# Row LSTM over group-normalised images: held row transfers, unread products tied to statistics, and a last step in two parts

## The chip, the core and the metric

The kernel runs on one core of a Trainium2 chip. A core has TensorE (matrix products, results in PSUM banks), VectorE, ScalarE, GpSimd (all three elementwise, GpSimd without access to PSUM) and SyncE, whose queue here issues every DMA. The metric is the device time of one launch in microseconds (us); lower is better. Six runs of the kernel before gave a median of 2072.43 us, from 2069.31 to 2076.78.

## The reference

`x` has 8 images of 96 channels, 128 rows, 128 columns, in float32. It is group-normalised over whole images (32 groups of 3 channels), and a row LSTM goes down the rows: a masked convolution of the normalised row, plus a convolution of the previous hidden row, gives four gates.

```python
def step(carry, row_in):
    h, c = carry
    ss = lax.conv_general_dilated(h, W_ss, window_strides=(1,), padding=((1, 1),), ...) + b_ss[None, :, None]
    gates = ss + row_in
    g5 = gates.reshape(B, 3, 4, Oc, Wd)
    f = jax.nn.sigmoid(g5[:, :, 0].reshape(B, O, Wd))
    i = jax.nn.sigmoid(g5[:, :, 1].reshape(B, O, Wd))
    o = jax.nn.sigmoid(g5[:, :, 2].reshape(B, O, Wd))
    g = jnp.tanh(g5[:, :, 3].reshape(B, O, Wd))
    c_new = f * c + i * g
    h_new = o * jnp.tanh(c_new)
    return ((h_new, c_new), h_new)
...
x = x + _L0_conv_ref(_gn(x), ...)
```

No hidden row can begin before the statistics of its image are complete, and the rows of one image follow each other.

## The kernel before

**Two halves.** The 8 images are two sets of four (`s` = 0 and 1). A half-step is one row of one set, so there are 256 of them, taken in turn: half-step `n` is row `n // 2` of set `n % 2`. One set's elementwise work runs while TensorE multiplies for the other. Each row is split into even and odd columns and the convolution is done with sums and differences: `vs` (total), `vf` (difference), `vd` (shifted differences) come from the hidden row with the last 32 normalised channels below it (`hx`); `xs` holds the same three for the first 64 channels.

**First stage: the statistics.** The loop at L700 to L728 reads each image as six chunks of 128 partitions x 2048 (1 MB; the last chunk in two halves) into a ring of six buffers, and VectorE runs `bn_stats` on 512 columns at a time (L724). Chunks 2 and 4 of an image are summed by ScalarE instead (`sums_of`, L209). The counter `m` counts pieces of 512, and `events` holds what is issued after piece `at(image, n)`: the whole preparation of half-steps 0 and 1 is written between the statistics of images 3 to 7. All engines but SyncE run in the order in which the program is written (`manual_schedule`); SyncE issues DMAs in program order too.

For set 1 the scale of its first three images is made at `at(7, 5)` to `at(7, 8)`; `next_row` (L625) normalises row 0 of these on GpSimd, `next_operands` (L631) makes their `vs`, `vf`, `vd` on GpSimd, and `own_row` at `at(7, 20)` their `xs`. The last image's scale can only follow the last `bn_stats`: `aggregate(7)`, then L735 to L744 (small matmuls L245 for deviations, variances and means, a Newton iteration for the reciprocal root on VectorE), then L745 to L758 for its row 0.

**Unread products.** `spin(count, rhs)` (L169) issues matmuls of 128 x 256 into a PSUM bank that nothing reads. There are 11 at `at(7, 8)` and 4 at L740, each of two passes on TensorE.

**Row transfers.** After the statistics loop SyncE issues, in this order: rows 1 to 3 of set 1 (`load_rows(1, 0, 1, R)` at L731: two transfers of 384 KB into the first and the last 64 partitions of `xr[1]`; `load(1, 0, 1, R)`: 192 KB and 576 KB into `x`), and then rows of the next block of four: `load_rows(0, 1)`, `load` of both sets, `load_rows(1, 1)` (L765 to L768). None of the first four waits for compute. ScalarE widens rows 1 to 3 of `xr[1]` (L761), GpSimd normalises their shared channels (L762) and combines them (L764); half-step 3 is the first to use the result.

**Second stage.** `do(1, ...)` at L771 begins the recurrent products, and the loop at L772 issues `PERIOD` for each `n`; a prime marks work of the half-step before. A half-step's last part is `gated` (i*g), `cell` (f*c + i*g), `cell_tanh`, `output`, and `residual` with the store in `finish`.

Of the kernel before, what the change touches and what calls it, by code (L numbers as in the profile page):

```python
# [8 lines left out]
AF = mybir.ActivationFunctionType  # L9
# [6 lines left out]
def strided(ap, offset, dims):  # L16

    return bass.AP(ap.tensor, ap.offset + offset, [ap.ap[0], *[list(d) for d in dims]])
# [3 lines left out]
def kernel(  # L22
# [32 lines left out]
    nc = tc.nc  # L55
    B, C, H, W = x.shape
    P = 128
    NH = 2
    BH = B // NH
# [25 lines left out]
    wt = [tap[1], wm[:, 0, :], wm[:, 1, :], tap[2]]  # L85
# [39 lines left out]
    xr = [const.tile([P, BH, R * W], F32, tag=f"xr{s}", name=f"xr{s}") for s in range(NH)]  # L125
# [3 lines left out]
    xw = [const.tile([P, R, W + 1], F32, tag=f"xw{i}", name=f"xw{i}") for i in range(2)]  # L129
# [21 lines left out]
    def load(s, k, lo=0, hi=R, copy=True):  # L151
        if lo == 0:
            xt[s, k] = x_pool.tile([P, BH, R, W], F32, tag=f"x{s}", name=f"x{s}_{k}")
        flat = xt[s, k].rearrange("c b r w -> c b (r w)")[:, :, lo * W : hi * W]
        if copy:
            nc.sync.dma_start(flat[C:P], rows_of(s, k, C2, C, lo, hi))
        nc.sync.dma_start(flat[0:C], rows_of(s, k, 0, C, lo, hi))
# [7 lines left out]
    def bank(name):  # L165
        return ps_pool.tile([P, 512], F32, tag="ps", name=name)


    def spin(count, rhs):  # L169
        unread = bank("spin")  # L170
        for i in range(count):
            nc.tensor.matmul(  # L172
                unread[:, 0 : rhs.shape[1]],
                wt[0][:, 0:P],
                rhs,
                start=True,
                stop=True,
                skip_group_check=True,
            )
# [113 lines left out]
    def widen(engine, xw, i, n, s, k, j, lo, step=1):  # L293


        norm(
            engine,
            strided(xw[:, i, :], 0, [(step * (W + 1), n), (J + 1, 2), (1, J)]),
            (x0[:, 0, j] if s == 1 and k == lo == 0 else xr[s][:, j, lo * W : (lo + n) * W])
            .rearrange("p (r j t) -> p r t j", r=n, t=2),  # L300
            0,
            1,
            s * BH + j,
        )

    def combine(xw, n, total, differences):

        e, o = xw[:, 0:n, 0:J], xw[:, 0:n, J + 1 :]
        nc.gpsimd.tensor_add(total, e, o)  # L309
        nc.gpsimd.tensor_sub(  # L310
            differences,
            strided(xw[:, 0, :], 0, [(W + 1, n), (J, 2), (1, J)]),
            strided(xw[:, 0, :], J + 1, [(W + 1, n), (0, 2), (1, J)]),
        )
# [7 lines left out]
    def own_row(xw, s, r, lo=0, hi=BH):  # L322

        to = xs[s][0]
        combine(
            xw[:, lo:hi],
            hi - lo,
            to[:, r, 0, lo:hi],
            to[:, r, 1:3, lo:hi].rearrange("p t b j -> p b t j"),
        )  # L330
# [24 lines left out]
    class HalfStep:  # L355
# [89 lines left out]
            to = self.g if self.row > 0 else self.c  # L445
            nc.vector.tensor_mul(to, self.ps[1][0:C], self.g)  # L446

        def cell(self):
            if self.row > 0:
                nc.vector.tensor_add(self.c, self.ps[0][0:C], self.g)  # L450

        def cell_tanh(self):
            self.th = self.tile("th")
            nc.scalar.activation(self.th, self.c, AF.Tanh)  # L454

        def output(self):
            s, row = self.s, self.row
            nxt = hx[s][(row + 1) // R % 2][0:C, (row + 1) % R]
            self.h = strided(nxt[:, 0, 0, :], 0, [(BH * JP + 1, 2), (JP, BH), (1, J)])
            shaped = "p (t b j) -> p t b j"  # L460
            nc.vector.tensor_mul(
                self.h,
                self.ps[2][0:C].rearrange(shaped, t=2, b=BH),
                self.th.rearrange(shaped, t=2, b=BH),
            )


        def operand(self, name, parts=1):
# [37 lines left out]
    def store(s, k, lo, hi):  # L506
        nc.sync.dma_start(
            out[s * BH : (s + 1) * BH, :, k * R + lo : k * R + hi, :].rearrange(
                "b c r w -> c b (r w)"
            ),  # L510
            xt[s, k][0:C, :, lo:hi, :].rearrange("c b r w -> c b (r w)"),
        )
# [21 lines left out]
    def work(n):  # L534
        if n < len(FIRST):
            return FIRST[n]
        row, s = divmod(n, NH)
        k, r = divmod(row, R)
        parts = []
        if r == R - 1 and k + 2 < NB:  # L540
            parts.append((own_image, s, k + 2, 0))
        elif r < R - 1 and k + 1 < NB:
            parts.append((own_image, s, k + 1, r + 1))
        if k + 1 < NB:
            parts += shared(s, k + 1, *SHARED[r])
        if r == R - 2 and k + 2 < NB:
            parts.append((load_rows, s, k + 2))
        return parts

    def finish(n):  # L550
        for part, *args in work(n):
            part(*args)
        row, s = divmod(n, NH)
        k, r = divmod(row, R)
        if r == R - 1:
            store(s, k, R - 1 if k + 1 == NB else 0, R)
            if k + 2 < NB:
                load(s, k + 2)
        elif r == R - 2 and k + 1 == NB:
            store(s, k, 0, R - 1)  # L560
# [19 lines left out]
    last = NT * NH - 1  # L580

    def half_step(n):
        if n not in steps:
            steps[n] = HalfStep(n)
        return steps[n]

    def do(n, names):

        for name in names.split():
            at = n  # L590
            for mark, offset in (("'", -1), ("+", 1), ("*", 2)):
                if mark in name:
                    at, name = n + offset, name.replace(mark, "")
            tile_ = name[-1] if name[-1] in order else ""
            part = name[: len(name) - len(tile_)]

            if part in ("S", "F", "D"):
                at += NH
            if not 0 <= at <= last:
                continue  # L600
            step = half_step(at)
            if name not in step.done:
                step.done.add(name)
                getattr(step, PARTS[part])(*([order[tile_]] if tile_ else []))
# [15 lines left out]
    def shared_rows(engine, s, lo, hi, images=range(BH)):  # L620
        for j in images:
            normalise_shared(engine, s, 0, j, lo, hi)


    def next_row():  # L625
        late[0].scale()
        late[0].shift()
        for j in range(BH - 1):
            widen(nc.gpsimd, xw[1], j, 1, 1, 0, j, 0)

    def next_operands():  # L631
        shared_rows(nc.scalar, 1, 0, 1, range(BH - 1))
        step = half_step(1)
        step.total(nc.gpsimd, 0, BH - 1)
        step.difference(nc.gpsimd, 0, BH - 1)
        step.shifted(0, BH - 1)

# [12 lines left out]
    def at(image, n):  # L650
        return image * NS + n
# [9 lines left out]
    def squares():  # L661
        late[0].squares()
        late[0].variances(late[0].q)
        late[0].means()


    events = {
        at(3, 1): lambda: first_rows(0, (0,)),
# [14 lines left out]
        at(6, 22): lambda: first_rows(1),  # L683
        at(7, 5): lambda: (late.insert(0, Scale(1, BH - 1, BH)), begin_scale(1, 0, BH - 1)),
        at(7, 6): squares,
        at(7, 8): lambda: (next_row(), spin(11, wt[0][:, 0:256])),
        at(7, 12): next_operands,
        at(7, 20): lambda: own_row(xw[1], 1, 0, 0, BH - 1),
    }
    for b in range(B - 1):  # L690
        events[at(b + 1, 7 if b == 4 else 4)] = lambda b=b: aggregate(b)
# [7 lines left out]
    n = m = 0  # L699
    for b in range(B):  # L700
        bst = g_pool.tile([P, NS, 6], F32, tag="bst", name=f"bst{b}")
# [4 lines left out]
        done = 0  # L706
# [30 lines left out]
    final.variance_and_square()  # L737
    final.variances(final.q)
    final.means()
    spin(4, wt[0][:, 0:256])  # L740
    nc.scalar.activation(final.minus, final.pm, AF.Identity, scale=-1.0)
    final.scale()
    nc.gpsimd.tensor_mul(final.nmr, final.minus, final.rstd)
    j = BH - 1  # L744
# [8 lines left out]
    step = half_step(1)  # L753
# [15 lines left out]


    do(1, "1A 2A 1B 2B PA PB QA QB PC P+A QC")  # L771
    for n in range(1, last + 2):  # L772
        for names in PERIOD:
            do(n, PRODUCTS[n % 2] if names == "X" else names)
            if "re'" in names.split():
                finish(n - 1)


# [53 lines left out]
```

## Time and profile before

The profiled execution took 2073.84 us; its span, from the first to the last instruction, is 2071.6 us.

| Quantity | Value |
|---|---|
| Median of 6 runs | 2072.43 us (2069.31 to 2076.78) |
| Profiled execution, time | 2073.84 us |
| Profiled execution, span | 2071.6 us |
| TensorE busy, share of the span | 1953.6 us, 94% |
| VectorE, GpSimd, ScalarE busy | 81%, 70%, 66% |
| Mean granted TensorE clock | 0.993 |
| First statistics to the last `bn_stats` | until 137.1 us |
| Recurrent products on TensorE | about 144 to 2064 us |

The page gives busy times and shares of each engine, the chain of work that ended last, and the costliest groups of instructions. Other views list instructions in order of time with the idle time before them and what ended it (in square brackets), or busy time, granted TensorE clock and DMA rate in stretches of the span. A granted clock of 1.00 is full speed, 0.50 half. In a row such as `L724 DVE ... x4`, L724 is the line of the program, DVE is VectorE, ACT ScalarE, POOL GpSimd, PE TensorE, and SPq SyncE's queue; PEld is TensorE loading weights.

### The profile page before, as it was taken

What the parts mean: (1) busy time and instruction counts of PE and PEld (TensorE: products, weight loads), DVE (VectorE), ACT (ScalarE), POOL (GpSimd) and SP (SyncE); (2) the same over time, 40 slices, a digit from 0 to 9 for tenths busy, and PEclk for the clock granted to TensorE, in tenths of its full rate; (3) what the DMA queues carried; (4) which work ended last, traced back from release to release, by engine and by line L of the source; (5) the groups of instructions that cost most, each with busy time, mean ns of one, the idle gap of its engine ahead of it and who ended that gap; (6) DMA issues with size and microseconds to landing.
All of it is one profiled execution on the core that took longest, in us unless ns stands there. A gap on an engine that the chain in (4) does not pass through costs nothing.

```text
span 2071.6 us, 31323 instructions
## 1 busy us (share of the span) xinstructions
PE 1953.6 (94%) x10832; PEld 1594.9 (77%) x10832; DVE 1678.0 (81%) x3491; ACT 1359.9 (66%) x2397; POOL 1443.7 (70%) x1645
## 2 busy tenths in 40 slices
PE   0259999999999999999999999999999999999998
PEld 0248888888888888888888888888888888888886
DVE  4768888888888888888888888888888888888887
ACT  4756666666666666666666666666666666666666
POOL 2347777777777777777777777777777777777762
PEclk9979999999999999999999999999999999999999
DMA  9993333444333344433334443333444333344411
GB/s 370 421 314 81 88 88 98 112 112 109 76 81 92 92 112 113 112 80 79 88 92 112 112 113 90 76 80 92 112 112 112 92 78 85 87 108 112 112 31 31
DMA packets 103324, 236.24 MB, mean 114 GB/s; under 512 B 5952, under 2 KB 8896, under 8 KB 97280
## 3 DMA queue, kind: packets, MB, share of 16 engines
q1 hardware_dynamic: 103168, 234.25, 41.4%
q8 instruction: 87, 1.43, 0.3%
q14 instruction: 69, 0.57, 0.1%
HBM read 183.90 MB, written 50.33 MB: 113 GB/s over the span
## 4 chain that ended last, share of the span: by engine, by line
PE 93%; DMA 4%; DVE 1%; POOL 0%; ACT 0%; SPq 0%; issue 0%; DVEq 0%; POOLq 0%
PE ps L378 93%; DMA xs<-in_x_dram 4%; DVE bst L724 1%; PE spin L172 0%; POOL xw L291 0%; POOL xs L310 0%; SPq L712 0%; POOL xs L309 0%; ACT xs L216 0%; ACT xs L215 0%; ACT g L430 0%; PE dm L245 0%; DVE g L446 0%; DVE c L450 0%; DVE st L654 0%
## 5 line engine op out<-in xcount | busy, mean ns | idle before, releaser
L378 PE MATMUL ps<-vd,wl 128*128 128x256 f32 x3072 | 815.6, 388 | 0.0
L430 ACT ACTIVATE g<-ps 32x512 f32<-32x512 f32 x768 | 453.7, 591 | 453.0 <-PE ps L378 444.6
L378 PEld LDWEIGHTS ps<-vd,wl 128*128 128x128 f32 x3072 | 563.7, 190 | 150.3 <-issue 85.4
L486 POOL TENSOR_TENSOR vd<-hx 128x512 f32<-128x512 f32 x257 | 266.2, 1036 | 469.2 <-DVE vs L478 466.2
L378 PE MATMUL ps<-xs,wx 64*128 64x256 f32 x3072 | 457.9, 395 | 10.7 <-POOL xs L309 10.7
L378 PE MATMUL ps<-vs,wm 128*128 128x256 f32 x1536 | 458.8, 381 | 0.0
L378 PE MATMUL ps<-vf,wm 128*128 128x256 f32 x1536 | 458.4, 380 | 0.0
L437 ACT ACTIVATE ps<-ps 96x512 f32<-96x512 f32 x766 | 417.5, 572 | 16.4 <-PE ps L378 0.3
L378 PEld LDWEIGHTS ps<-xs,wx 64*128 64x128 f32 x3072 | 323.4, 187 | 118.5 <-issue 84.4
L442 DVE TENSOR_TENSOR ps<-ps,c 96x512 f32<-96x512 f32 x254 | 176.8, 696 | 261.6 <-ACT ps L437 261.6
L427 DVE TENSOR_TENSOR ps<-m,ps 128x256 f32<-128x256 f32 x768 | 329.3, 429 | 26.4
L423 DVE TENSOR_TENSOR ps<-m,ps 128x256 f32<-128x256 f32 x768 | 325.3, 424 | 9.4 <-ACT m L420 0.7
L504 POOL TENSOR_TENSOR x<-x,hx 96x512 f32<-96x512 f32 x254 | 328.7, 1294 | 0.0
L378 PEld LDWEIGHTS ps<-vs,wm 128*128 128x128 f32 x1536 | 293.2, 191 | 40.2 <-POOL vs L478 0.7
L378 PEld LDWEIGHTS ps<-vf,wm 128*128 128x128 f32 x1536 | 293.0, 191 | 39.6 <-DVE vf L482 0.3
L420 ACT ACTIVATE m<-ps,wl 128x256 f32<-128x256 f32 x513 | 243.2, 474 | 77.1 <-PE ps L378 63.6
L310 POOL TENSOR_TENSOR xs<-xw 128x512 f32<-128x512 f32 (+1 forms) x254 | 269.9, 1063 | 0.0
L378 PE MATMUL ps<-xs,wt 64*128 64x256 f32 x1536 | 264.9, 377 | 0.1
L454 ACT ACTIVATE th<-c 96x512 f32<-96x512 f32 x256 | 161.2, 630 | 106.2 <-DVE c L450 105.1
L291 POOL TENSOR_SCALAR hx<-x,rstd,nmr 32x512 f32<-32x512 f32 (+1 forms) x252 | 203.4, 807 | 25.9
L378 PEld LDWEIGHTS ps<-xs,wt 64*128 64x128 f32 x1536 | 195.3, 187 | 18.4 <-issue 1.0
L291 POOL TENSOR_SCALAR xw<-xr,rstd,nmr 128x512 f32<-128x512 f32 x252 | 203.6, 808 | 7.0 <-DVE nmr L283 6.5
(84 smaller groups left out, 1283.0 us busy)
## 6 DMA issues: line engine op xcount, KB each, us to landing
xr<-in_x_dram SPq DMA_DIRECT2D x124, 512.0 KB, 6.4
x<-in_x_dram SPq DMA_DIRECT2D x63, 768.0 KB, 5.8
out_dram<-x SPq DMA_DIRECT2D x62, 768.0 KB, 4.7
xs<-in_x_dram SPq DMA_DIRECT2D x30, 1024.0 KB, 12.4
piece<-in_x_dram SPq DMA_DIRECT2D x16, 1024.0 KB, 12.4
x<-in_x_dram SPq DMA_DIRECT2D x62, 256.0 KB, 3.1
xs<-in_x_dram SPq DMA_DIRECT2D x4, 512.0 KB, 8.5
out_dram<-x SPq DMA_DIRECT2D x2, 576.0 KB, 3.7
```

The lines of the kernel that those rows point to most:

```text
L291: engine.tensor_scalar(dst, src, scale, shift, ALU.mult, ALU.add)
L310: nc.gpsimd.tensor_sub(differences, strided(xw[:, 0, :], 0, [(W + 1, n), (J, 2), (1, J)]), strided(xw[:, 0, :], J + 1, [(W + 1, n), (0, 2) ...
L378: nc.tensor.matmul(self.ps[a][:, bass.ts(half, HB)], weights[rows, bass.ts(a, P)], rhs[rows], start=new, stop=False, skip_group_check=True,)
L420: nc.scalar.activation(self.m1[a], m1, AF.Identity, bias=column)
L423: nc.vector.tensor_add(self.ps[a][:, 0:HB], self.m1[a], self.ps[a][:, HB:])
L427: nc.vector.tensor_sub(hi, self.m1[a], hi)
L430: nc.scalar.activation(self.g[a * 32 : (a + 1) * 32], self.ps[a][C:P], AF.Tanh)
L437: nc.scalar.activation(gate, gate, AF.Sigmoid)
L442: nc.vector.tensor_mul(f, f, self.c)
L454: nc.scalar.activation(self.th, self.c, AF.Tanh)
L486: diff = nc.gpsimd.tensor_sub(self.operand("vd", 2)[:, :, lo:hi], strided(h, 1, [(BH * JP - 1, 2), (JP, hi - lo), (1, J)]), strided(h, 0, ...
L504: (nc.gpsimd if row + 1 < NT else nc.vector).tensor_add(xo, xo, self.h)
```

## The change

Three parts, each at its own place.

- `next_operands` gets a GpSimd write of one column of zeros into `xr[1]`, behind the `total` of that step. The column is the first of row 1, so `load_rows(1, 0, 1, R)`, which writes over it, waits for it; GpSimd's `difference` and `shifted` come after it.
- The unread products at `at(7, 8)` go from 11 to 8. `keep_warm(count)` issues one product that reads the newest record of `bn_stats` (6 columns), in a bank of its own, and `count` products of the old kind in another. It is called with 2 at `at(7, 20)`, 2 at `at(7, 22)` and 1 at `at(7, 24)`: behind the last `bn_stats` of chunk 4, and of each half of chunk 5. The unread products at L740 go from 4 to 2.
- The half-step loop ends one turn earlier. What the last turn did for the last half-step is written out: the same products, sigmoids, tanhs and `gated`, then `cell` and `cell_tanh` for images 0 and 1 and for images 2 and 3, then `output` in the same two parts, `residual` and `finish`.

The built program's order agrees: TensorE has the new products in these places, GpSimd one Memset between `vs` and `vf`, the first row transfer waits for GpSimd, and the last half-step has two instructions each in place of one on VectorE (`c`, `hx`) and ScalarE (`th`). The order of all else is the same.

```diff
+        def part(self, ap, lo, hi):
+            return ap.rearrange("p (t b j) -> p t b j", t=2, b=BH)[:, :, lo:hi]
+
-        def cell(self):
+        def cell(self, lo=0, hi=BH):
             if self.row > 0:
-                nc.vector.tensor_add(self.c, self.ps[0][0:C], self.g)
-
-        def cell_tanh(self):
-            self.th = self.tile("th")
-            nc.scalar.activation(self.th, self.c, AF.Tanh)
-
-        def output(self):
+                c, f, g = (self.part(ap, lo, hi) for ap in (self.c, self.ps[0][0:C], self.g))
+                nc.vector.tensor_add(c, f, g)
+
+        def cell_tanh(self, lo=0, hi=BH):
+            if lo == 0:
+                self.th = self.tile("th")
+            nc.scalar.activation(self.part(self.th, lo, hi), self.part(self.c, lo, hi), AF.Tanh)
+
+        def output(self, lo=0, hi=BH):
...
-            shaped = "p (t b j) -> p t b j"
-            nc.vector.tensor_mul(
-                self.h,
-                self.ps[2][0:C].rearrange(shaped, t=2, b=BH),
-                self.th.rearrange(shaped, t=2, b=BH),
-            )
+            o, th = (self.part(ap, lo, hi) for ap in (self.ps[2][0:C], self.th))
+            nc.vector.tensor_mul(self.h[:, :, lo:hi], o, th)
...
         step.total(nc.gpsimd, 0, BH - 1)
+        nc.gpsimd.memset(xr[1][:, 0, W : W + 1], 0.0)
         step.difference(nc.gpsimd, 0, BH - 1)
...
+    def keep_warm(count):
+        spin(1, bst[:, done - 1, :])
+        spin(count, wt[0][:, 0:256])
...
-        at(7, 8): lambda: (next_row(), spin(11, wt[0][:, 0:256])),
+        at(7, 8): lambda: (next_row(), spin(8, wt[0][:, 0:256])),
         at(7, 12): next_operands,
-        at(7, 20): lambda: own_row(xw[1], 1, 0, 0, BH - 1),
+        at(7, 20): lambda: (own_row(xw[1], 1, 0, 0, BH - 1), keep_warm(2)),
+        at(7, 22): lambda: keep_warm(2),
+        at(7, 24): lambda: keep_warm(1),
...
-    spin(4, wt[0][:, 0:256])
+    spin(2, wt[0][:, 0:256])
...
-    for n in range(1, last + 2):
+    for n in range(1, last + 1):
         for names in PERIOD:
             do(n, PRODUCTS[n % 2] if names == "X" else names)
             if "re'" in names.split():
                 finish(n - 1)
+    do(last, "siB fg taB 3C 0C taC siC gt")
+    step, halves = half_step(last), [(0, BH // 2), (BH // 2, BH)]
+    for at in halves:
+        step.cell(*at)
+        step.cell_tanh(*at)
+    for at in halves:
+        step.output(*at)
+    step.residual()
+    finish(last)
```

## The prediction, made before the changed kernel ran

> **What bounds the kernel now.** I read the engine shares first, then the chain of work that ended last, then the stretches where that chain is not TensorE's steady work. The page's summary of the chain:
>
> ```profile
> PE 93%; DMA 4%; DVE 1%; POOL 0%; ACT 0%; SPq 0%; issue 0%; DVEq 0%; POOLq 0%
> ```
>
> 93% is one unbroken run of matmuls, from about 144 us to 2058 us. The change leaves it alone. What can move is when that run starts and the 13 us behind it. The chain around the start (start, duration, what):
>
> ```profile
> 120.89 14.91 DMA xs<-in_x_dram
> ...
> 135.82 1.30 DVE bst L724 x2
> ...
> 137.21 0.68 DVE st L654
> ...
> 138.03 0.57 PE dm L245 x2
> ...
> 138.62 0.29 DVE q L266
> ...
> 138.96 1.02 PE pv L245 x4
> 139.98 0.85 PE dm L245 x4
> 140.83 3.42 PE spin L172 x8
> 144.25 5.79 PE ps L378 x31
> ```
>
> The start is held in three places: by the last image transfer, by small matmuls for the last image's scale, and by the four unread products (eight passes, 3.42 us). VectorE's timeline shows the first:
>
> ```profile
> 131.16 1.29 DVE L724 BATCH_NORM_STATS2 bst<-xs 128x6 f32<-128x512 f32 x2 [0.41 <-DMA xs<-in_x_dram]
> 132.88 1.29 DVE L724 BATCH_NORM_STATS2 bst<-xs 128x6 f32<-128x512 f32 x2 [0.43 <-DMA xs<-in_x_dram]
> 135.82 1.28 DVE L724 BATCH_NORM_STATS2 bst<-xs 128x6 f32<-128x512 f32 x2 [1.66 <-DMA xs<-in_x_dram]
> ```
>
> These are the last chunks' statistics. The first 512 KB half of the last chunk is there at 132.88, the second only at 135.82. Why, and what TensorE's clock does, stands in the table by stretches (us, busy time of PE, PEld, DVE, ACT, POOL, granted clock, DMA share, GB/s):
>
> ```profile
> 120.00:126.00 6.00, 2.07 (x10) 2.04 (x10) 5.87 (x13) 1.94 (x4) 0.26 (x1) 0.50 1.01 421
> ...
> 131.00:137.00 6.00, 2.63 (x13) 1.97 (x11) 3.75 (x6) 3.09 (x6) 3.93 (x10) 1.00 1.09 208
> ```
>
> ```profile
> 133.67:137.09 3.42, 0.00 (x0) 0.00 (x0) 1.76 (x3) 0.51 (x2) 2.07 (x8) 1.00 1.08 198
> 137.09:140.50 3.41, 2.10 (x10) 2.04 (x10) 1.39 (x6) 0.00 (x0) 0.00 (x0) 0.50 1.10 218
> 140.50:143.91 3.41, 3.41 (x10) 2.78 (x11) 1.58 (x9) 2.09 (x5) 1.50 (x5) 0.50 1.07 222
> ```
>
> With image chunks alone the queues move 421 GB/s; from 131 us, with row transfers among them (issued from 121.3 us on, into 64, 32 or 96 partitions), 208 GB/s at a full DMA share. And after a stretch with no matmul at all the clock is 0.50 until 143.91.
>
> **Part 1: the rows held.** SP issues in order, so the first row transfer waits for GpSimd's new one-column write and the ten behind it wait too. Image chunks stand ahead and are untouched. 512 KB at 421 GB/s is 1.25 us, so the second half would land at 134.1, by when VectorE has just finished the first half (132.88 + 1.29 = 134.17). The statistics then end near 135.4 instead of 137.1: 1.7 us. If the first half also comes sooner, VectorE can close its 0.43 us too; the bound is 2.1 us. The lower bound is 0, if the late half was late by itself. I take 1.8, near the upper end, because the rate row changes just where the rows join in.
>
> The write itself is 0.10 us (memset rows of L217) behind the sum at L478:
>
> ```profile
> 131.81 0.53 POOL L478 TENSOR_TENSOR vs<-hx 128x192 f32<-128x192 f32 x1 [1.22 <-ACT hx L289]
> ```
>
> So the rows are released near 132.45, 11 us after their issue before. What is late next: ScalarE's four widenings of the rows, then GpSimd's.
>
> ```profile
> 142.33 3.03 ACT L289 ACTIVATE piece<-xr,nmr,rstd 128x384 f32<-128x384 f32 x4
> 147.11 0.47 ACT L420 ACTIVATE m<-ps,wl 128x256 f32<-128x256 f32 x1 [1.76 <-PE ps L378]
> ```
>
> The page has 6.4 us from issue to landing for one 512 KB transfer of this kind, in pairs, in the steady stage; two of 384 KB should take no more, so they land at about 138.8. If they share the queues with the 768 KB of x rows behind them, 1.57 MB at 213 GB/s is 7.4 us, plus 1.9 us around it (the page's 256 KB x transfer lands in 3.1 us, 1.2 of them at that rate): 141.8. ScalarE will ask at 142.33 - 2.6 = 139.7 (2.6 us from parts 1 and 2) and is followed in its queue by the copy of L420. That copy had 1.76 us of idle time, of which part 3 takes 1.6, and its reader on VectorE (the pair at 148.39) came 0.8 us after it ended. So a start until 140.6 costs nothing and 141.8 costs 1.2 us. I take 0, as 138.8 has the page's own row behind it; 1.2 goes into the range. GpSimd's shared rows (143.63 before) wait for the third transfer, with its first result asked for by TensorE near 151 and made at 147.4: 3.6 us of slack less 1.6. The next user, GpSimd at 151.68 with the next block's rows, needs 2.6 MB: 12.3 us at 213 GB/s, so about 147 against 149 after the shift. Even late, that work is for half-step 8.
>
> The Trainium skill speaks against this part: "DMA: Bandwidth & Descriptors", Rules for kernel authors, says to issue a DMA early and wait late, so that its fixed cost (about 2.0 us in its anatomy section) overlaps. By that rule the hold exposes 2.0 us with no gain, and the whole change would bring an estimated 1.8 + 2.0 = 3.8 us less than the sum below; the row of 208 against 421 GB/s shows a price of issuing early that the rule leaves out, so I go by the row.
>
> **Part 2: products tied to bn_stats.** The eleven products at one event become eight; five more follow in three groups, and each group begins with a six-column product that reads the newest statistics record, so it can't run before VectorE got there. Groups would run at about 132.5, 133.9 and 135.4, with gaps of a microsecond at most, in place of an empty stretch. The rows above give 2.10 us of matmuls in a stretch that stayed at 0.50, so such groups would not raise the clock; do they keep it? At the end of the kernel the clock falls at 2069.03 although TensorE's last matmul ends at 2063.6, so a stretch of 3.41 us with 1.4 us of matmuls (2062.2 to 2065.6) kept it. I take it that it stays at 1.0. The price of the small matmuls then: eight passes (L245, pv<-eps at 105.23) take 0.95 us at clock 1.0, 0.12 each; four take 1.02 us at 0.50, 0.25 each. On the path are two passes before q and four before rstd: 6 x 0.13 = 0.8 us. Bounds: 0 if the clock falls, 0.8 if it stays. Queued behind the last group on TensorE is the matmul that reads st: two small and two large passes, 0.24 + 0.43 = 0.7 us, beside 0.68 us of aggregation. Cost nothing at clock 1.0, 0.7 at 0.50. The three groups take six more PSUM banks in turn; their earlier owners ended before 111 us.
>
> **Part 3: two unread products instead of four.** VectorE has the first real operands ready here:
>
> ```profile
> 142.18 0.22 DVE L482 TENSOR_TENSOR vf<-hx 128x64 f32<-128x64 f32 x1
> ```
>
> That ends at 142.40, and TensorE took its first real product at 144.08. With four passes at 0.21 us (0.43 at half clock) TensorE is free before that operand is, so the start follows the operand: 144.08 - 142.40 less 0.08 for the handover is 1.6 us. The operands after that (own rows by 143.16, shifted differences by 143.52, minus 2.6) come before their turns: eight passes of the first four products take 1.7 us.
>
> **Part 4: the last cell in two parts.** The end of the chain before:
>
> ```profile
> 2065.38 0.70 DVE c L450
> ...
> 2066.10 0.64 ACT th L454
> ...
> 2066.77 0.70 DVE hx L461
> ```
>
> That is 2.09 us with handovers. A 256-element VectorE operation takes 0.43 us (rows L423 and L427, against 0.69 for 512). For half a tanh the rows give 0.47 (L420, 256 elements) at most and 0.32 at least (half of 0.63); I take 0.42. Chain: cell 0.43, cell 0.43, with the second tanh from 0.89 to 1.31 and the second output to 1.77. Saved 0.3 us, bounds 0.2 and 0.45. The residual waits for both, as before.
>
> **The sum.** 1.8 + 0.8 + 1.6 + 0.3 = 4.5 us. The profiled execution had a span of 2071.6 and a time of 2073.84, so it would become 2067.1 and 2069.3. It lies 1.4 above the median of the six runs, 2072.43; from that the forecast is 2067.9.
>
> **Rivals.** *The clock falls all the same* (nothing shows a gap of a microsecond after groups this small). Then part 2 gives -0.1 instead of 0.8, and the real products start cold, with too few unread ones left to warm it: two full stretches of 3.41 us at most, half of which is lost, at least 0.9 us and at most 2.6. With 1.8 lost, 4.5 - 0.9 - 1.8 = 1.8 us gain: 2070.6. For it: the cold stretches 137.09 to 143.91. Against: the end of the kernel.
>
> *The late half was late anyway*, by its own queue: part 1 gives 0, the gain is 2.7, 2069.7. For it: that half was issued last. Against: 1.25 us at the full rate does not make 2.9.
>
> *The held rows come too late* (the slower side). ScalarE's widenings stand ahead of L420 in its queue, so rows after 140.6 push TensorE one for one. Before, these transfers took 16.8 us to land. If that is their own time and not their place behind the image, they land at 149.3, 8.7 us past the free point: 4.5 - 8.7 = 4.2 us slower, 2076.6. It decides from a landing after 145.1. Against: 6.4 us for larger ones on the page.
>
> *More than forecast*: in this execution the clock rose at 143.91, 0.17 us before the first real product. Where the stretches fall later, the kernel before starts cold by up to 3.4 us and loses up to 1.7; gain 6.2, 2066.2.
>
> **How the numbers follow.** Forecast 0.54, more 0.10, clock 0.14, late half anyway 0.14, rows late 0.08. What a measurement of this kernel can tell from no change is about 0.2%, 4.1 us. The forecast's 4.5 lies just past it: of its 0.54 I put 0.43 past and 0.11 within. Faster 0.43 + 0.10 = 0.53; same 0.11 + 0.14 + 0.14 = 0.39 and 0.01 of the rows; slower 0.07. The range goes from 2064.4 (6.2 plus the runs' own scatter) to 2072.2, which takes in the clock rival, the rows' 1.2 us and the smaller part 1, and leaves out the slow case.
>
> **What would show it.** After: the wait of 1.66 us before the last statistics gone or under 0.5; no row packets before about 133; DMA idle a microsecond there; clock 1.0 from 130 us through the start; first real product near 139.8, straight after vf; no idle time on ScalarE's L289 rows nor a longer one before L420. A dark stretch of the clock after 133, ScalarE waiting on a DMA past 140.6, or a first product that waits on an unread one, each proves one step wrong.

## The result, and the profile after

The changed kernel takes 2068.38 us (median of 21 runs, 2066.1 to 2072.96) against 2072.48 us before (42 runs): a ratio of 0.9979, with a 95% interval from 0.9973 to 0.9985. That is 4.1 us less by the medians, 3.1 to 5.6 by the interval. The forecast was 4.5 us less, 2067.9 us.

The profiled execution has a span of 2065.1 us, 6.5 less than that of before. Not all of this is the change: VectorE begins the statistics of the last image's chunk 3 at 126.57 us where it was 128.28 before, and nothing that VectorE waits for ahead of that point is changed. Eleven of the twelve profiles below have it between 125.9 and 127.1, with the change or with parts of it, so the profile of before was late there by about 1.7 us of its own. What remains, about 4.7 us, divides like this:

| Stretch | Before, us | After, us | Less, us |
|---|---|---|---|
| A: first `bn_stats` of chunk 3 to the end of the last one | 8.83 | 6.28 | 2.55 |
| B: from there to the first `rstd` operation | 2.91 | 2.56 | 0.35 |
| C: from there to the first real product | 4.07 | 2.39 | 1.68 |
| D: first real product to the end of the last one | 1919.56 | 1919.63 | -0.07 |
| E: from there to the end of the span | 7.91 | 7.68 | 0.23 |

VectorE's timeline after (start, duration, engine, instruction, and idle time ahead of it in brackets):

```profile
126.57 2.47 DVE L735 BATCH_NORM_STATS2 bst<-piece 128x6 f32<-128x512 f32 x4
129.08 3.77 DVE L735 BATCH_NORM_STATS2 bst<-xs 128x6 f32<-128x512 f32 x6
132.96 0.67 DVE L659 BATCH_NORM_AGGREGATE st<-bst 128x2 f32<-128x114 f32 x1
134.44 0.28 DVE L266 TENSOR_SCALAR q<-dm,st 128x1 f32<-128x1 f32 x1 [0.81 <-PE dm L245]
```

The three waits of before (0.41, 0.43, 1.66 us) are gone: the last six statistics run as one row without a gap. Stretch A is now VectorE's own time. The stretches (us, busy PE, PEld, DVE, ACT, POOL, granted clock, DMA share, GB/s) show the hole that the hold leaves, and the clock:

```profile
131.10:132.10 1.00, 1.00 (x7) 0.92 (x6) 1.00 (x2) 0.97 (x3) 1.00 (x4) 1.00 0.00 0
133.66:137.08 3.42, 2.77 (x17) 2.17 (x16) 1.59 (x10) 0.17 (x1) 0.58 (x2) 1.00 1.11 213
137.08:140.49 3.41, 2.68 (x16) 2.16 (x18) 0.69 (x3) 3.06 (x5) 2.57 (x6) 1.00 1.12 224
```

For one microsecond the queues move nothing, between the last image packet and the first row packet; the clock is 1.00 throughout, where it was 0.50 from 137.09 to 143.91. The rows are there when ScalarE wants them:

```profile
137.73 3.02 ACT L289 ACTIVATE piece<-xr,nmr,rstd 128x384 f32<-128x384 f32 x4
140.92 0.47 ACT L420 ACTIVATE m<-ps,wl 128x256 f32<-128x256 f32 x1 [0.17 <-PE ps L378]
```

The widenings start with no wait, and L420's idle time fell from 1.76 to 0.17 us, as the forecast's sum of spare time has it. The chain around the start (start, duration, what):

```profile
125.48 8.80 PE spin L172 x32
134.29 0.13 PE dm L245 x2
...
134.44 0.29 DVE q L266
...
134.78 0.62 PE pv L245 x4
...
137.67 0.15 DVE vf L484
137.81 12.26 PE ps L378 x66
```

Two things are to be seen. The first real product now follows `vf`, not an unread product. But the unread products stand in the chain all the same, at another place: 8.80 us of them run back to back until 134.29, and the matmul on `st`, ready at 133.63, is behind them.

### The profile page after: what moved, and what is told of

Read it like the earlier page. It is cut to its first block, busy times and chain, and to the rows that moved or that the text cites. A ratio compares the mean times of both kernels' runs of the same rounds, so it can differ in the third digit from the quotient of the medians.

```text
span 2065.1 us, 31343 instructions
## 1 busy us (share of the span) xinstructions
PE 1951.8 (95%) x10838; PEld 1593.6 (77%) x10838; DVE 1677.2 (81%) x3493; ACT 1359.7 (66%) x2398; POOL 1445.2 (70%) x1646
## 3 DMA queue, kind: packets, MB, share of 16 engines
q8 instruction: 88, 1.44, 0.3%
## 4 chain that ended last, share of the span: by engine, by line
PE 94%; DMA 4%; DVE 1%; POOL 0%; ACT 0%; issue 0%; SPq 0%; DVEq 0%; POOLq 0%
PE ps L378 93%; DMA xs<-in_x_dram 4%; DVE bst L735 1%; PE spin L172 0%; POOL xw L291 0%; POOL xs L310 0%; SPq L723 0%; POOL xs L309 0%; PE pv L245 0%; ACT xs L216 0%; ACT xs L215 0%; ACT g L430 0%; PE dm L245 0%; DVE g L446 0%; DVE c L455 0%
## 5 line engine op out<-in xcount | busy, mean ns | idle before, releaser
L420 ACT ACTIVATE m<-ps,wl 128x256 f32<-128x256 f32 x513 | 243.1, 474 | 74.9 <-PE ps L378 61.3
L460 ACT ACTIVATE th<-c 96x512 f32<-96x512 f32 (+1 forms) x257 | 161.3, 628 | 106.6 <-DVE c L455 104.6
```

Of the source, the lines that this page charges most:

```text
L420: nc.scalar.activation(self.m1[a], m1, AF.Identity, bias=column)
L460: nc.scalar.activation(self.part(self.th, lo, hi), self.part(self.c, lo, hi), AF.Tanh)
```

## The experiments

Each was timed beside the kernel before: e1 to e4, e5 to e8 and e9 to e12 on one chip each, where the kernel before had medians of 2073.10, 2072.87 and 2072.91 us. Across these groups the ratios are to be compared, not the medians. The table has all twelve; A to D are the stretches above, and the last column says where the profiled execution's clock fell to 0.50 near the start. E is 7.67 to 7.69 us in every profile with the split, and 7.89 to 7.91 in the three without it.

| Kernel | Median, us | Ratio, 95% interval | A | B | C | D | Clock lost, us |
|---|---|---|---|---|---|---|---|
| e1 hold alone | 2069.41 | 0.9982 [0.9973, 0.9990] | 6.98 | 2.29 | 3.76 | 1919.57 | 136.29 to 139.70 |
| e2 unread products alone | 2070.49 | 0.9989 [0.9980, 0.9997] | 9.04 | 3.34 | 2.52 | 1920.16 | 135.70 to 142.53 |
| e3 split alone | 2072.79 | 0.9997 [0.9988, 1.0006] | 10.01 | 2.90 | 4.00 | 1919.58 | 136.70 to 143.53 |
| e4 write too early | 2070.51 | 0.9989 [0.9980, 0.9997] | 7.85 | 2.29 | 2.39 | 1920.26 | 136.33 to 139.74 |
| e5 rows late | 2075.06 | 1.0008 [1.0000, 1.0017] | 7.09 | 2.29 | 2.46 | 1924.38 | 137.57 to 144.39 |
| e6 no groups | 2069.05 | 0.9982 [0.9973, 0.9991] | 6.25 | 2.31 | 2.40 | 1920.31 | 137.34 to 140.76 |
| e7 groups 1, 1, 1 | 2068.74 | 0.9981 [0.9972, 0.9990] | 6.28 | 2.29 | 2.40 | 1921.21 | 137.02 to 140.44 |
| e8 7, then 3, 3, 1 | 2067.30 | 0.9976 [0.9966, 0.9986] | 6.28 | 2.71 | 2.40 | 1919.66 | not |
| e9 changed, again | 2067.01 | 0.9978 [0.9970, 0.9987] | 6.28 | 2.73 | 2.40 | 1921.05 | 136.90 to 140.31 |
| e10 hold and split | 2069.08 | 0.9981 [0.9973, 0.9990] | 6.84 | 2.30 | 3.56 | 1919.78 | 136.05 to 139.46 |
| e11 as e8 | 2067.29 | 0.9974 [0.9965, 0.9983] | 6.29 | 2.72 | 2.40 | 1919.65 | not |
| e12 7, then 3, 3, 0 | 2067.17 | 0.9978 [0.9969, 0.9987] | 6.28 | 2.46 | 2.39 | 1922.55 | 136.55 to 143.38 |

### The three parts, each alone

**e1, the hold alone.**

```diff
         step.total(nc.gpsimd, 0, BH - 1)
+        nc.gpsimd.memset(xr[1][:, 0, W : W + 1], 0.0)
         step.difference(nc.gpsimd, 0, BH - 1)
```

> The kernel before plus GpSimd's one-column write alone; unread products and last half-step as before. Theory (row packets in front of the last image packets made the second half late): from the first bn_stats of the last image's chunk 3 to the end of the last bn_stats 6.3 us in place of 8.8, clock and start of the products as before (about 4 us from the first rstd operation to the first real product, 0.50 clock before it), time 2.0 to 2.5 us below before. Rival (the late half is scatter of one execution): that stretch stays between 8 and 9 us, time within 0.7 us of before.

Measured: 3.7 us less (2.1 to 5.6 by the interval), where 2.0 to 2.5 was expected; the profile has 2.8 (1.85 in A, 0.62 in B, 0.31 in C). The late half is no scatter: A is 6.98 us here, against 8.83 to 10.01 in the three profiles where the rows are not held at all (before, e2, e3). VectorE's statistics and the stretches of e1:

```profile
129.97 3.79 DVE L725 BATCH_NORM_STATS2 bst<-xs 128x6 f32<-128x512 f32 x6 [0.72 <-DMA xs<-in_x_dram]
```

```profile
132.87:136.29 3.42, 1.23 (x10) 1.18 (x10) 2.04 (x6) 0.00 (x0) 1.59 (x4) 1.00 1.05 235
136.29:139.70 3.41, 3.41 (x10) 2.78 (x10) 1.80 (x10) 1.88 (x4) 1.24 (x5) 0.50 1.12 238
```

The waits for both halves of the last chunk are gone; the 0.72 us that are left stand ahead of chunk 4, of whose four pieces VectorE has two in the last image. The second surprise is B, 2.29 us with the old unread products. The clock was simply still up: the last statistics end at 133.76 us, 2.5 us before the clock falls, where before they ended together with the fall (137.11 and 137.09). So the hold by itself earns most of what the forecast booked under the groups.

**e2, the unread products alone.**

```diff
+    def keep_warm(count):
+        spin(1, bst[:, done - 1, :])
+        spin(count, wt[0][:, 0:256])
...
-        at(7, 8): lambda: (next_row(), spin(11, wt[0][:, 0:256])),
+        at(7, 8): lambda: (next_row(), spin(8, wt[0][:, 0:256])),
...
+        at(7, 20): lambda: (own_row(xw[1], 1, 0, 0, BH - 1), keep_warm(2)),
+        at(7, 22): lambda: keep_warm(2),
+        at(7, 24): lambda: keep_warm(1),
...
-    spin(4, wt[0][:, 0:256])
+    spin(2, wt[0][:, 0:256])
```

> The kernel before plus the new unread products alone (8, three groups tied to bn_stats, 2); no hold, last half-step as before. Theory: the clock stays at 1.00 from about 130 us on though the groups lie up to 3 us apart; from the end of the last bn_stats to the first rstd operation 2.5 us in place of 2.9, from there to the first real product 2.4 in place of 4.1; time 1.8 to 2.2 us below before. Rival (groups this small keep no clock without the hold, which brings them close together): a stretch at 0.50 between 134 and 144 us and real products in it, time 0 to 1.5 below before, or above it.

Measured: 2.3 us less by the ratio, but by other terms than the theory's. The rival's mark is there, in the stretches of e2:

```profile
132.29:135.70 3.41, 1.39 (x7) 1.00 (x7) 1.40 (x3) 0.07 (x1) 1.62 (x5) 1.00 1.10 201
135.70:139.12 3.42, 3.04 (x13) 2.78 (x13) 1.10 (x4) 0.00 (x0) 0.00 (x0) 0.50 1.12 216
```

Without the hold the last half is 2 us late, the groups lie apart, and a stretch with 1.39 us of matmuls lost the clock. B grew to 3.34 us, as the last group runs at half speed ahead of the matmul on `st`. In the profile the gain is C alone, 2.52 us instead of 4.07, and the other stretches take most of it back: the five together are only 0.3 us less than those of before, and A to D 1.4 less than in e3. The interval of the time goes from 0.6 to 4.1 us; where the rest of the 2.3 comes from stays open.

**e3, the split alone.** `cell`, `cell_tanh` and `output` in two parts, nothing else of the change.

> The kernel before plus the last half-step's cell and output in two parts alone. Theory: from the last product's end to the end of the span 7.66 us in place of 7.90, time 0.2 to 0.3 below before, which is less than such a comparison can tell from nothing. Rival (the split changes nothing, the store behind it sets the end): 7.90 stays.

Measured: ratio 0.9997, which tells nothing, as expected. E is 7.69 us, close to the theory's 7.66 and not the rival's 7.90. The end of the chain of the changed kernel:

```profile
2059.18 0.43 DVE c L455
...
2059.63 0.42 ACT th L460
...
2060.08 0.43 DVE hx L467
...
2060.60 0.43 DVE hx L467
```

These are the forecast's 0.43 and 0.42; the second output starts 0.09 us behind the first.

### The hold: too early and too late

**e4, the write too early.** The changed kernel with the same one-column write at the head of `next_row`.

```diff
     def next_row():
+        nc.gpsimd.memset(xr[1][:, 0, W : W + 1], 0.0)
...
         step.total(nc.gpsimd, 0, BH - 1)
-        nc.gpsimd.memset(xr[1][:, 0, W : W + 1], 0.0)
```

> The changed kernel with the one-column write put ahead of next_row, where GpSimd runs it some 3 us earlier; the wait on GpSimd is the same, all else too. Theory (what counts is that no row packet flows before the last image packet): rows are released near 127 and meet the last image packets again, the stretch from the first bn_stats of chunk 3 to the last one's end goes from 6.3 back to 8 to 8.8 us, time 1.5 to 2.5 above the changed kernel, so 2 to 2.5 below before. Rival (any wait of the row transfers on GpSimd does it, or the order of issue): 6.3 us stays, time 4 below before.

GpSimd was idle there and ran the write at 118.04 us, so the release came not near 127 but before 119.03, when SyncE issued the first row transfer: the wait is in the program and holds nothing. Measured: 2070.51 us, 2.1 above the changed kernel's 2068.38 (also 2.1 by the ratios). VectorE's timeline of e4:

```profile
128.49 2.56 DVE L735 BATCH_NORM_STATS2 bst<-xs 128x6 f32<-128x512 f32 x4
132.54 1.29 DVE L735 BATCH_NORM_STATS2 bst<-xs 128x6 f32<-128x512 f32 x2 [1.48 <-DMA xs<-in_x_dram]
```

The wait for the second half is back, 1.48 us, and the ratio is that of e2, which has no hold. So what counts is when the rows flow, not that they wait.

**e5, the rows late.** The release moved behind the last scale, with two more one-column writes, so that the rows of set 1 and the next block's first ones wait there.

```diff
-        nc.gpsimd.memset(xr[1][:, 0, W : W + 1], 0.0)
...
-    load_rows(1, 0, 1, R)
-    load(1, 0, 1, R)
...
     nc.gpsimd.tensor_mul(final.nmr, final.minus, final.rstd)
+    nc.gpsimd.memset(xr[1][:, 0, W : W + 1], 0.0)
+    nc.gpsimd.memset(xt[1, 0][:, 0, 1, 0:1], 0.0)
+    nc.gpsimd.memset(xr[0][:, 0, 0:1], 0.0)
+    load_rows(1, 0, 1, R)
+    load(1, 0, 1, R)
```

> The changed kernel with the release moved behind the last image's scale on GpSimd (three one-column writes there, so that the first row transfers and the next block's first ones wait), about 6.5 us later than in the changed kernel. Theory (ScalarE's widenings wait for the rows and hold up the copy of L420 behind them; about 1 us is free): rows land near 143 to 145, widenings start 5 to 7 us after the 0.05 us gap they have now behind the last image's row, TensorE idles 3 to 6 us between 139 and 152, time 3 to 6 above the changed kernel, so -1 to +2 against before. Rival (there is more room, since the first use of the rows by TensorE is half-step 3): time within 1 of the changed kernel, 4 below before.

Two transfers of the next block (1 MB, set 0) went ahead of the held ones. Measured: 2075.06 us, a ratio of 1.0008 [1.0000, 1.0017] to before, 6.0 above the changed kernel by the ratios. ScalarE's timeline, and TensorE's one long wait:

```profile
144.14 3.05 ACT L289 ACTIVATE piece<-xr,nmr,rstd 128x384 f32<-128x384 f32 x4 [5.96 <-DMA xr<-in_x_dram]
147.10 0.81 ACT L420 ACTIVATE m<-ps,wl 128x256 f32<-128x256 f32 x2
```

```profile
148.53 0.70 PE L378 MATMUL ps<-vd,wl 128*128 128x256 f32 x2 [1.48 <-DVE ps L427]
```

This is the forecast's slower rival, brought about on purpose: rows 5.96 us late, L420 behind the widenings, D longer by 4.8 us. TensorE idles only 1.48 us of that, less than the 3 to 6 expected; nearly all the rest are passes at half clock, from 138.24 to 144.39. They lie ahead of the same wait for L420's result, so at full clock that wait would, by these times, have been longer by as much; no run has the late rows without the fall. About one microsecond of the six is free, which is what the spare time left.

### The groups: what they earn, and what decides the clock

**e6, no groups.** 8 unread products, then 2; the three `keep_warm` calls left out.

> The changed kernel without the three groups tied to bn_stats (8 unread products, then 2). Theory (a stretch of 3.41 us with 2 us of matmuls or less loses the clock): 0.50 from about 136 us through the start of the real products, last bn_stats to first rstd operation 2.9 in place of 2.56, first real products at half speed for 1 to 4 us, time 0.8 to 2 above the changed kernel. Rival (the groups earn nothing, since they stand ahead of the matmul on st and the clock falls with them too): within 0.5 of the changed kernel.

Measured: 2069.05 us, 0.6 above the changed kernel by the ratios; the intervals overlap, so the time doesn't settle what the groups earn. The profile has the theory's 0.50 from 137.34 us and D longer by 0.7, but not its B: 2.31 us, as in e1, because B lies before the fall.

**e7, groups of 1, 1 and 1.**

> The changed kernel with 1, 1 and 1 old products in the groups in place of 2, 2 and 1. Theory A (the groups' queue delays the matmul on st): that matmul starts 0.1 us after st in place of 0.5, time 0.3 to 0.5 below the changed kernel. Theory B (fewer products lose the clock): 0.50 in the stretch where the real products start, time 0.3 to 1.5 above it.

Measured: 2068.74 us, 0.4 above the changed kernel. In the profile both theories hold: B is 2.29 us (the matmul on `st` starts 0.14 us after it, with no queue ahead of it) and the clock is lost at 137.02, which makes D longer by 1.6. The time is too close to the changed kernel's to tell either way.

**e8 and e11, 7 and then 3, 3 and 1.**

```diff
-        at(7, 8): lambda: (next_row(), spin(8, wt[0][:, 0:256])),
+        at(7, 8): lambda: (next_row(), spin(7, wt[0][:, 0:256])),
...
-        at(7, 20): lambda: (own_row(xw[1], 1, 0, 0, BH - 1), keep_warm(2)),
-        at(7, 22): lambda: keep_warm(2),
+        at(7, 20): lambda: (own_row(xw[1], 1, 0, 0, BH - 1), keep_warm(3)),
+        at(7, 22): lambda: keep_warm(3),
```

> The changed kernel with 7 unread products at first and 3, 3 and 1 in the groups. Theory (2.7 us of matmuls in a stretch keep the clock, 2.0 do not): no stretch at 0.50 between 130 us and the end, the matmul on st delayed by 0.5 to 0.9 us where the groups run back to back, time from 0.5 below to 0.3 above the changed kernel and less scatter over its runs. Rival (the clock falls all the same): a stretch at 0.50 near 136 to 140, time 0.5 above it.

> The kernel with 7 unread products at first and 3, 3 and 1 in the groups again, now beside the changed kernel. Theory (it keeps the clock in every execution): 2067 to 2067.6, 0.5 to 1.5 below the changed kernel, no execution over 2069.5. Rival (its lead was scatter): within 0.4 of the changed kernel.

Measured: 2067.30 and 2067.29 us, 19 runs between 2066.55 and 2068.79, none with a mean clock under 0.993. The changed kernel has runs up to 2072.96, and of its 22 recorded runs in the first comparison (one more than in the median above) 7 had a mean clock of 0.992 (median 2070.0) and 10 had 0.994 (2067.5). The medians don't separate: e9, on e11's chip, has 2067.01, so that e11 is not the 0.5 to 1.5 us below it that was expected. No faster kernel is shown, but one with less scatter, whose clock didn't fall in either profile.

**e9, the changed kernel again**, beside e10 to e12.

> The changed kernel once more, beside the next three on one chip. Theory (its time depends on where the clock's stretches fall): 2067 to 2069.5, with executions of about 2066.5 where the clock holds and of 2069 and more where it falls.

Measured: 2067.01 us, and this time the profile caught the clock falling. The stretches of e9:

```profile
133.48:136.90 3.42, 2.58 (x16) 1.99 (x15) 1.77 (x10) 0.17 (x1) 0.41 (x3) 1.00 1.07 208
136.90:140.31 3.41, 2.85 (x7) 2.32 (x8) 0.51 (x3) 3.24 (x5) 2.48 (x7) 0.50 1.11 236
```

and TensorE's timeline there:

```profile
135.33 1.11 PE L172 MATMUL spin<-wl 128*128 128x256 f32 x4
137.46 1.19 PE L378 MATMUL ps<-vs,wm 128*128 128x256 f32 x2 [1.02 <-DVE vf L484]
138.44 1.06 PE L378 MATMUL ps<-vf,wm 128*128 128x256 f32 x2
```

The same kernel, the same instructions: here the first real products ran at half speed (0.43 us a pass, not 0.21) until 140.31, and D is 1.4 us longer than in the first profile.

**e10, the hold and the split, with the old unread products.**

> The changed kernel with the old unread products (11, then 4, no groups): the hold and the split alone. Theory (the hold alone already brings the last statistics into the stretch that the 11 products keep warm, so the parts overlap): 2068.5 to 2069.5, 0.5 to 1.5 above the changed kernel, last bn_stats to first rstd operation 2.3 us, first rstd operation to first real product 2.4 where the clock holds through the four products, 3.5 to 4.1 where it falls. Rival (the parts add up as forecast, 2.4 us for the unread products): 2070 to 2071.

Measured: 2069.08 us, 3.9 us under before by the ratio, the theory's value. So the three parts don't add: by the ratios the hold alone has 3.7 (e1), the hold with the split 3.9 and the new unread products alone 2.3 (e2), but all together only 4.4 to 4.6 (0.9979, 0.9978). What the unread products add on top of the hold is 0.5 to 0.7 us by the ratios and 2.1 by the medians on one chip (2067.01 against 2069.08); the intervals overlap. What the hold adds to the new unread products is 2.1 us by the ratios (0.9979 against 0.9989 in e2 and in e4), also with overlapping intervals: the times show each by itself, the profiles what each does beside the other.

**e12, the last group without its large product.**

```diff
-        at(7, 24): lambda: keep_warm(1),
+        at(7, 24): lambda: spin(1, bst[:, done - 1, :]),
```

> The same with 3, 3 and 0: the last group is the six-column product alone. Theory (the last group's products delay the matmul on st by 0.4 us where the groups run back to back): from st to q 0.5 us in place of 0.9, time 0.2 to 0.4 below the kernel with 3, 3 and 1, as long as the clock holds. Rival (the last group is needed for the clock): a stretch at 0.50 near 136, time 0.3 to 1 above it.

Measured: 2067.17 us, in two heaps: 7 runs from 2066.3 to 2067.6 with a mean clock of 0.993 or 0.994, and 4 from 2069.4 to 2070.3 with 0.992. Both have their part: B is 0.26 us shorter than in e11, and the clock falls now and then. In the profile it fell for two stretches, 136.55 to 143.38, and D is 2.9 us longer.

## Why the prediction was right

**Part 1 (1.8 us taken, bound 2.1): right in mechanism, somewhat small in size.** A measured 2.55 less in the two profiles. Of this 0.41 is VectorE's wait ahead of chunk 4, which is not shown to be the hold's: before, it ended at 131.16 us, when the first row packet began (131.17), and e1 and e10 have 0.72 and 0.58 us there with the rows held. Without it the two profiles have 2.1, the bound; e3's, the other one with old products and no hold, waited 1.31 and 1.44 us for the two halves, 2.75 in all. e4 and e1 show the cause: the late half comes and goes with the time at which row packets begin. The forecast gave as reason that the image's packets flow more slowly; they do, and the landing behind the last of them is late too (the last section has both).

**The price of the hold (0 taken, 0 to 1.2): right.** The first two row transfers took 5.2 us to land, under the 6.4 that was used; the widenings didn't wait. By e5 the spare time is about a microsecond, and the slower rival is real from there on. The page that the prediction quotes against the hold gives its 2.0 us for transfers issued from GpSimd, while SyncE issues these; no run here measures that cost, and the loss estimated from it did not show: e1 gained.

**Part 2 (0.8 us taken): the weakest step, 0.35 measured.** The question whether such groups keep the clock was answered with the end of the kernel, a stretch with 1.45 us of matmuls that kept it. That case lies on the border: the same stretch at the end of e1, 1.39 us busy, lost it. In the profile of after the clock was kept; in e2, e4, e5 and e9 the same groups lost it. That it held in the profile of after is luck. And the 0.8 is not the groups' to give: B is 2.3 us in e1, e6 and e7, with the old products, no groups and small ones, since the hold alone moves the last scale ahead of the fall. The groups make B longer (2.56, and 2.73 in e9), because they run back to back and stand ahead of the matmul on `st`. The forecast had "cost nothing at clock 1.0" for this queue; it cost 0.3 to 0.4 us, and e12, without the last group's large product, has 0.26 of that back:

```profile
133.47 0.28 PE L172 MATMUL spin<-bst,wl 128*128 128x6 f32 x2
133.61 0.68 PE L172 MATMUL spin<-wl 128*128 128x256 f32 x2
134.12 0.28 PE L245 MATMUL dm<-st,wl 128*128 128x1 f32 x2
```

The third group's statistics were ready at 132.85 us and its product ran at 133.47, as the eight products before it had only ended at 131.46. What a kept clock earns lies behind the first real product: 0.7 us (D in e6) to 2.9 (e12's two lost stretches). In the times of whole runs the groups' share is not clear of noise.

**Part 3 (1.6 us taken): right, 1.68.** The start follows `vf` by 0.01 us. C is 2.39 to 2.52 us in every profile with two products there and 3.56 to 4.07 in the four with four; but those four ran them at half clock. Whether four at full clock would have held up the start was not run; by the rows of after (eight passes of 0.21 us from 135.69) they would end near 137.6, ahead of `vf` at 137.80.

**Part 4 (0.3 us taken): right within its bounds, 0.23.**

**The sum.** 2.55 + 0.35 + 1.68 - 0.07 + 0.23 = 4.7 us in the profiles against 4.5, and 4.1 in the medians. Part 1 was low by 0.75 and part 2 high by 0.45; that they nearly cancel is luck. So is it that the sum came out although its parts overlap: by the ratios the hold alone is worth 3.7 us, twice its term. That the medians lie lower fits the clock rival, given 0.14 for the whole: it happens in some executions of the same kernel (2070.0 against 2067.5 us above), so it is not a case beside the forecast but a share of its runs. That it explains the whole difference is not shown.

## What to carry to other kernels

When a stage ends with a stream into all 128 partitions and transfers into fewer are queued right behind it, look at the last wide transfer's landing: the others, if not needed yet, can be held by a cheap write to a place that they overwrite. Their release has a window: a write that ran too early was worth nothing (e4), and by e5's times there was about a microsecond to spare on the late side. Unread products meant to keep a clock need enough columns in every stretch, wherever the stretches fall, and they belong where nothing on the path queues behind them. Parts of a change that move the same moment don't add: run each alone.

## What the runs showed of the hardware

**The clock's threshold.** The clock changes only on a grid of 3.41 us, which lies at another place in each execution. From the matmul records of all fourteen profiles, from 100 us on, one can count the time for which columns stream: 0.21 us for a pass of 256 at full clock, twice that at half clock, in proportion for small ones. Here each pass is placed at the end of its record; placed at the start, the bounds move by about 0.2 us. From full clock, every stretch with under 1.2 us of it was followed by 0.50 and every one with over 1.5 by 1.00. Between, both occur: 1.29 kept it in the changed kernel and lost it in e9, 1.23 (e5), 1.38 (e12) and 1.48 (e3, from 102.57 us) lost it, 1.20 kept it in e8. From half clock, at most 2.4 us brought no rise and 2.6 or more did. Products of 1 or 6 columns count as busy time in the views but hardly stream: e12's stretch of 2.87 us busy lost the clock and e11's of 2.39 kept it:

```profile
133.14:136.55 3.41, 2.87 (x19) 2.28 (x17) 1.75 (x10) 0.17 (x1) 0.82 (x2) 1.00 1.11 221
136.55:139.96 3.41, 2.56 (x6) 2.12 (x7) 0.71 (x3) 2.94 (x5) 2.45 (x6) 0.50 1.11 236
```

```profile
132.31:135.73 3.42, 3.04 (x20) 2.75 (x21) 1.65 (x4) 0.17 (x2) 1.76 (x5) 1.00 1.00 230
135.73:139.14 3.41, 2.39 (x12) 1.84 (x12) 1.86 (x11) 1.78 (x4) 1.21 (x4) 1.00 1.10 228
```

By streaming time they are 1.38 (e12, from 133.14) and 1.76 (e11, from 135.73). This rule was found after the runs and no run was made to test it.

**Row transfers delay the image transfer ahead of them, in two ways.** In the profile of before the 4 KB packets of the last image chunk took 0.16 us each until row packets began at 131.17 us, and then up to 0.48 us; from the first to the last of them it is 6.2 us, and 5.8 and 6.8 in e2 and e3. In the changed kernel it is 3.9 us, none took over 0.18, and the last ended 1.0 us before the first row packet. The second way is the landing. With row packets on the queues VectorE was let go 0.97 us (before), 1.18 (e2), 1.31 (e3) and 1.51 (e4) after the last image packet had ended. In the nine profiles with the rows held behind the image it began the last half's statistics 0.44 to 0.47 us after that packet, without a wait. In e4 the packets themselves took 3.9 us, so there the landing alone brings the wait back. Why it is late was not tried, nor whether the rows' fewer partitions or their smaller packets (1.5 KB) do the slowing.
